# Layer 0's last three blocks and layer 3's last one: results added by one-hot matmuls instead of scatters

## The chip, the cores and the metric

The kernel runs on one core of a Trainium2 chip. The core has five engines with a queue of instructions each: TensorE (PE, with its weight loads as PEld), VectorE (DVE), ScalarE (ACT), GpSimd (POOL) and SyncE (SP). SP, ACT and POOL can start DMA transfers; 16 DMA engines carry them. The metric is the time of one execution on the device, in microseconds (us), lower is better. Times below that are not called medians come from one profiled execution and count from the start of its span.

## The reference

A model of four layers on 1024 tokens (4 sequences of 256) of width 256, all in float32. Each layer normalises the residual, adds a gated attention, normalises again, and adds a gated feed-forward part:

```python
x = x + tanh(g_xattn[0]) * L0_xattn(layernorm(x), ctx_512, ...)
x = x + tanh(g_ffn[0])   * L0_ffn(layernorm(x), ...)
...
x = x + tanh(g_xattn[3]) * L3_xattn(layernorm(x), ctx_512, ...)
x = x + tanh(g_ffn[3])   * L3_ffn(layernorm(x), ...)
```

Two of the feed-forward parts are mixtures of experts. Layer 0 has 16 experts of width 176 with 6 chosen for each token, and two shared ones; layer 3 has 8 experts of width 512 with 2 chosen, and one shared:

```python
# layer 0, for every expert
h = silu(x @ W1.T + B1) * (x @ W3.T + B3)
y = y + c[:, None] * (h @ W2.T + B2)      # c: the token's weight for this expert, or 0
# layer 1's feed-forward part: weights reduced to -1, 0 and 1
scale = mean(abs(w)); w_q = sign(w) * (abs(w) >= 0.7 * scale)
```

## The kernel before

The residual lies in SBUF as `stream`, 8 tiles of 128 tokens by 256 (`x[t]` is one). All steps are written one after the other and a scheduler places each engine's instructions.

**A mixture** (`ffn0`, `ffn3`) first routes: for each token and chosen expert it computes a place in a list sorted by expert, and cuts that list into blocks of 128 places, each with one expert. The class `Experts` runs over the blocks. For block `b`: `fetch` gathers 128 rows of the normalised tokens and their weights from DRAM with an indirect DMA on GpSimd (L1152); `turn` transposes them (L1164, copied by VectorE in L1165) and picks each row's weight (L1170); `up` multiplies with the expert's first weights (L1193, in layer 3 L1204), takes silu on ScalarE (L1212) and multiplies on VectorE (L1213); `turn_hidden` transposes the result (L1219, L1221); `down` multiplies with the second weights (L1228) and copies the result to one of 8 places of a ring in SBUF (L1237 on VectorE for odd blocks, L1239 on ScalarE for even ones). Then an indirect DMA on GpSimd adds the 128 rows to an accumulator in DRAM (L1240). Layer 0 alternates between two accumulators, `sums0[0]` (which starts as a copy of the residual) and `sums0[1]` (which starts as zero); layer 3 has one, `sums3[0]`. Two scatters to the same accumulator wait for one another.

`blocks` fetches four blocks ahead and keeps three blocks in work, so that in iteration `i` block `i` is turned, block `i-1` goes up and block `i-2` down; then it calls `between(i)`. Layer 0's `between` lets other work into the mixture: at every third iteration a step of `fold1` (TensorE folds weights of layer 1's attention, and the steps release weight buffers, so that the next loads start on SP), and after iteration 32 a step of `ternary1` (VectorE reduces and rounds the two weight matrices of layer 1's feed-forward part: eight `tensor_reduce` in L1462, a small matmul for the mean in L1472, then eight comparisons and eight selects in L1481 and L1482).

How many blocks there are depends on the data. 55 in layer 0 and 20 in layer 3 are sure; the rest stands behind a branch (`tc.If` on a value loaded in L1251). Every engine has its own copy of that branch, and on the path that skips the rest it raises its semaphores as if the rest had run; GpSimd does so for the scatters.

**After layer 0's mixture**, SP loads the first accumulator into `stream` (L1372) and ScalarE's queue loads the second into `more` (L1374), two loads of 512 KB each; VectorE adds them (L1377, four adds of two tiles); SP starts to load layer 3's expert weights once the adds are done; then layer 1's attention normalises the tiles (`layernorm`, L379 to L387), TensorE transposes them (L399) and projects them (L414, 16 projections of two matmuls), and softmax follows on VectorE, ScalarE and GpSimd (L420 to L430).

**At the end**, four copies from `sums3[0]` to the output, DRAM to DRAM, on SP and ScalarE (L1628).

`region`, `t4` and `small` take buffers of SBUF; `ps_mm` takes one of four PSUM banks.

Of the kernel before, what the change touches and what calls it, by code (L numbers as in the profile page):

```python
# [25 lines left out]
F32 = mybir.dt.float32  # L29
# [8 lines left out]
P = 128  # L38
# [27 lines left out]

NB0, NB3 = _blocks(E0, K0), _blocks(E3, K3)
SURE0, SURE3 = 55, 20
W0U = 4 * F0
W0, W3 = W0U + 2 * D, 4 * F3 + 4 * D  # L70
BIG = E3 * W3
# [10 lines left out]
def tile_flamingo(ctx: ExitStack, tc: tile.TileContext, a: dict, out: bass.AP):  # L82
# [291 lines left out]
    def layernorm(g):  # L374

        mv = small([P, TPG, 2], "mv")
        for i in range(TPG):
            st = small([P, 6], "st")
            nc.vector.bn_stats(st, x[g * TPG + i])  # L379
            nc.vector.bn_aggr(mv[:, i, :], st)  # L380
        rstd = small([P, TPG], "rstd")
        nc.scalar.activation(rstd, mv[:, :, 1], AF.Sqrt, bias=eps)  # L382
        nc.vector.reciprocal(rstd, rstd)
        xn = []
        for i in range(TPG):
            n = sb.tile([P, D], F32, tag="xn", name="xn", bufs=6)
            nc.vector.tensor_scalar(  # L387
                n, x[g * TPG + i], mv[:, i, 0:1], rstd[:, i : i + 1], ALU.subtract, ALU.mult
            )
            xn.append(n)  # L390
        return xn
# [432 lines left out]

    def attention1(gate):
        weff, wvo = kept.pop("fold1")
        qcT = latents()
        xT = [transposed(layernorm(0))]
        for g in range(NG):
            for pr in range(NP):  # L830
                if g == 0 and pr == NP // 2:
                    xT.append(transposed(layernorm(1)))
                ps = ps_mm()
                mm2(ps, lambda c: weff[:, c, pr * P : (pr + 1) * P], xT[g])
                evacuate(qcT[g][:, pr, :], ps)
        latent_attend(qcT, wvo, gate)


# [295 lines left out]
    class Experts:  # L1134


        def __init__(self, route, xd, n, nb, stride, width, chunk, sums, w, bias, hTs, between):
            self.gather, self.scatter, self.expert, self.offset, self.used = route
            self.xd, self.experts, self.nb, self.stride = xd, n, nb, stride
            self.width, self.chunk, self.n = width, chunk, width // chunk  # L1140
            self.sums, self.w, self.bias, self.hTs = sums, w, bias, hTs
            self.between = between
            self.ring = [sb.tile([P, 4, D], F32, tag="xT", name="ring", bufs=2) for _ in range(2)]
            self.weight: dict = {}
            self.xs: dict = {}
            self.at: dict = {}
            self.st: dict = {}
# [36 lines left out]
        def up(self, b):  # L1184
            st, r, n = self.st[b], self.at[b], self.width
            ps = ps_wide()
            s = st[:, D : D + n]
            if self.bias is not None:
                nc.tensor.matmul(
                    ps[:, 0, : 2 * n], self.bias[1][:, b : b + 1].to_broadcast([96, P]), self.bias[0], start=True, stop=False  # L1190
                )
                for c in range(2):
                    nc.tensor.matmul(  # L1193
                        ps[:, 0, : 2 * n],
                        st[:, c * P : (c + 1) * P],
                        self.w[:, bass.ds(r + c * 2 * n, 2 * n)],
                        start=False,
                        stop=(c == 1),
                    )
                gate, lin = ps[:, 0, :n], ps[:, 0, n : 2 * n]  # L1200
            else:
                for c in range(2):
                    for k in range(2):
                        nc.tensor.matmul(  # L1204
                            ps[:, k, :n],
                            st[:, c * P : (c + 1) * P],
                            self.w[:, bass.ds(r + (2 * c + k) * n, n)],
                            start=(c == 0),
                            stop=(c == 1),
                        )  # L1210
                gate, lin = ps[:, 0, :n], ps[:, 1, :n]
            nc.scalar.activation(s, gate, AF.Silu)  # L1212
            nc.vector.scalar_tensor_tensor(s, lin, self.weight.pop(b), s, ALU.mult, ALU.mult)  # L1213

        def turn_hidden(self, b):
            st, f = self.st[b], self.chunk
# [7 lines left out]
        def down(self, b):  # L1224
            (st, hT), r = self.st.pop(b), self.at.pop(b) + 4 * self.width
            ps = ps_mm()
            for j in range(self.n):
                nc.tensor.matmul(  # L1228
                    ps[:, :D],
                    hT[:, j * P : (j + 1) * P],  # L1230
                    self.w[: self.chunk, bass.ds(r + j * D, D)],
                    start=(j == 0),
                    stop=(j == self.n - 1),
                )
            y = self.ring[b // 4 % 2][:, b % 4, :]
            if b % 2:
                nc.vector.tensor_copy(y, ps[:, :D])  # L1237
            else:
                nc.scalar.copy(y, ps[:, :D])  # L1239
            nc.gpsimd.indirect_dma_start(  # L1240
                out=self.sums[b % len(self.sums)],
                out_offset=bass.IndirectOffsetOnAxis(ap=self.scatter[:, b : b + 1].bitcast(U32), axis=0),
                in_=y,
                in_offset=None,
                compute_op=ALU.add,
            )

        def run(self, sure):

            self.blocks(0, sure, self.between)  # L1250
            used = nc.values_load(self.used, min_val=0, max_val=self.nb)  # L1251
            with tc.If(used > sure):
                self.blocks(sure, self.nb, lambda i: None)

        def blocks(self, first, last, between):
            for b in range(first, min(first + 4, last)):
                self.fetch(b)
            for i in range(first, last + 2):
                if i + 4 < last:
                    self.fetch(i + 4)  # L1260
                if i < last:
                    self.turn(i)
                if i >= first + 2:
                    self.turn_hidden(i - 2)
                if first < i <= last:
                    self.up(i - 1)
                if i >= first + 2:
                    self.down(i - 2)
                between(i)

    def in_three(n, first, second, third):

# [5 lines left out]
    def ffn0(gate):  # L1278
# [60 lines left out]
        in_three(NT, up, turn, down)  # L1339
        for _ in steps:  # L1340
            pass
        used("L0_s13")
        used("L0_s2")
        keep_rows(sums0[0], 0)
        placing = route[1]
        expert = placing[2]
# [5 lines left out]

        fold = fold1()
        ended = []
        ternary = ternary1()

        def between(i):
            if i % 3 == 2 and not ended:
                try:
                    next(fold)  # L1360
                except StopIteration as end:
                    ended.append(end.value)
            if i > 32 and ended:
                next(ternary, None)

        moe = Experts(placing, xd, E0, NB0, W0, F0, FC0, sums0, big[:, : E0 * W0], (bias_0, choice), hTs, between)
        moe.run(SURE0)
        kept["fold1"] = ended[0]
        for t in range(NT):
            if t % TPG == 0:  # L1370
                tiles = slice(t, t + TPG)
                nc.sync.dma_start(out=stream[:, tiles, :], in_=tiled(sums0[0], 0)[:, tiles, :])  # L1372
                more = t4([P, TPG, D], "more")
                nc.scalar.dma_start(out=more, in_=tiled(sums0[1], 0)[:, tiles, :])  # L1374
            if t % 2 == 0:
                two, its = slice(t, t + 2), slice(t % TPG, t % TPG + 2)
                done = nc.vector.tensor_tensor(stream[:, two, :], stream[:, two, :], more[:, its, :], ALU.add)  # L1377
        load_experts3(0, EARLY3, done)
        for _ in ternary:
            pass  # L1380

    def ffn3(gate):
        normal = normalised()
# [53 lines left out]
        def hTs(st, b):  # L1437
            return hidden[:, (b % 4) * 512 : (b % 4 + 1) * 512]

        moe = Experts(route[0], xd, E3, NB3, W3, F3, P, sums3, big, None, hTs, lambda i: None)  # L1440
        moe.run(SURE3)


    def ternary(k):
# [10 lines left out]
    def ternary1():  # L1455
# [3 lines left out]
        for k in range(2):  # L1459
            part = small([P, 16], "part", 2)  # L1460
            for i in range(4):
                nc.vector.tensor_reduce(  # L1462
                    part[:, i * 4 : (i + 1) * 4],
                    loaded[f"L1_w{k + 1}"][:, i * 512 : (i + 1) * 512].rearrange("p (a b) -> p a b", a=4),
                    AX.X,
                    ALU.add,
                    apply_absolute_value=True,
                )
                yield
            nc.vector.tensor_reduce(sums[:, k : k + 1], part, AX.X, ALU.add)  # L1470
        ps = ps_mm()
# [149 lines left out]
        k = 4 * (i % 2) + i // 2  # L1621
        step(tg[:, k : k + 1])

    for i in range(4):
        rows = slice(i * T // 4, (i + 1) * T // 4)
        to, of = (v[rows].rearrange("(p r) d -> p (r d)", r=4) for v in (out, sums3[0]))
        engine = nc.scalar if i % 2 else nc.sync
        engine.dma_start(out=to, in_=of)  # L1628

def _rope(length, dim):
# [133 lines left out]
```

## Time and profile before

| | |
|---|---|
| median of 3 runs | 975.11 us (970.66, 975.11, 975.20) |
| profiled execution | 969.81 us |
| its span | 967.7 us |
| TensorE busy | 843.5 us (87%) |
| VectorE busy | 523.9 us (54%) |
| ScalarE busy | 274.1 us (28%) |
| GpSimd busy | 339.6 us (35%) |
| mean granted TensorE clock | 0.942 of full |

The rows of the profile read as follows. In a group, `out<-in` names the tiles by the program's names, then come shapes and the count; behind the first bar stand busy time and the mean of one in ns, behind the second the idle time of the engine just before and what ended it. In a timeline a row is start, length (us), engine, line, operation, tiles, count, and in brackets the idle time before it with its releaser. GpSimd's two kinds of work in layer 0's mixture:

```profile
L1240 POOL DMA_INDIRECT sums<-ring,big x55 | 87.8, 1596 | 34.4 <-issue 11.0
L1152 POOL DMA_INDIRECT xs<-xd,big x55 | 54.9, 999 | 55.9 <-DMA w_L_kv<-in_L_kv 35.5
```

The busy time of a group is a sum over all its instructions, whatever else runs beside them; a share of the span says nothing of whether the engine was waited for.

### The profile page before, as it was taken

The numbers are of one execution on the slowest core, as the hardware profiler recorded it, in microseconds if no ns is written. First come the engines' busy times: TensorE is split into PE (matmuls) and PEld (weight loads), VectorE is DVE, ScalarE is ACT, GpSimd is POOL, SyncE is SP. The second block draws the span as 40 slices with busy tenths as digits, with TensorE's granted clock in tenths as the row PEclk, the third lists the DMA queues.
The fourth block names the chain that finished last, engine by engine and source line by source line (L and its number), as shares of the span: only waits on it lengthen the run. The fifth ranks groups of instructions, "written<-read, shape, count | busy, mean of one in ns | idle before, by whom it ended". The sixth has DMA issues, their size and how long they took to land. (4 is left out here: it accounts for less than half of the span.)

```text
span 967.7 us, 12703 instructions
## 1 busy us (share of the span) xinstructions
PE 843.5 (87%) x4450; PEld 545.9 (56%) x4453; DVE 523.9 (54%) x1349; ACT 274.1 (28%) x531; POOL 339.6 (35%) x259
## 2 busy tenths in 40 slices
PE   5999999999999999984299987979647989999994
PEld 4544336876667866663147853835423556566662
DVE  4666557747833445361428745967796756222220
ACT  2122014443213232321113436134403441122221
POOL 0455552210157777886003124304201312144421
PEclk9999999999989999997599999988858999999998
DMA  9201137100266676554630000540000012122223
GB/s 346 96 16 39 60 123 220 33 28 9 77 150 161 127 169 149 86 83 57 231 121 1 1 1 0 184 154 2 22 1 1 1 44 52 45 45 44 39 22 66
DMA packets 38761, 75.14 MB, mean 78 GB/s; under 512 B 6240, under 2 KB 26706, under 8 KB 37322
## 3 DMA queue, kind: packets, MB, share of 16 engines
q1 hardware_dynamic: 23562, 52.01, 16.0%
q0 software_dynamic: 14496, 20.47, 13.2%
q10 hardware_dynamic: 640, 1.84, 0.5%
q8 instruction: 39, 0.64, 0.3%
q14 instruction: 24, 0.20, 0.1%
HBM read 58.73 MB, written 16.61 MB: 78 GB/s over the span
## 5 line engine op out<-in xcount | busy, mean ns | idle before, releaser
L430 POOL TENSOR_TENSOR attn<-attn,sm 128x1024 f32<-128x1024 f32 x32 | 60.8, 1901 | 242.3 <-DVE sm L429 224.3
L1213 DVE SCALAR_TENSOR_TENSOR blk<-wide,weight,blk 128x176 f32<-128x176 f32 (+1 forms) x75 | 37.0, 493 | 129.7 <-ACT blk L1212 122.8
L1240 POOL DMA_INDIRECT sums<-ring,big x55 | 87.8, 1596 | 34.4 <-issue 11.0
L414 PE MATMUL wide<-xT,big 128*128 128x512 f32 x192 | 87.9, 607 | 0.0
L675 DVE TENSOR_TENSOR rope<-wide,big 128x512 f32<-128x512 f32 x96 | 59.6, 684 | 48.3 <-PE wide L414 47.1
L1193 PE MATMUL wide<-big,blk 128*128 x220 | 76.1, 467 | 0.0
L1152 POOL DMA_INDIRECT xs<-xd,big x55 | 54.9, 999 | 55.9 <-DMA w_L_kv<-in_L_kv 35.5
L1204 PE MATMUL wide<-big,blk 128*128 x160 | 72.2, 593 | 0.5 <-DVE blk L1165 0.5
L399 PE MATMUL mm<-ident,xn 128*128 128x128 f32 x112 | 21.7, 342 | 52.7 <-DVE xn L387 40.4
L1212 ACT ACTIVATE blk<-wide 128x176 f32<-128x176 f32 (+1 forms) x75 | 29.5, 393 | 121.7 <-PE wide L1204 52.6
L414 PEld LDWEIGHTS wide<-xT,big 128*128 128x128 f32 x192 | 35.6, 193 | 47.1 <-issue 41.2
L648 PE MATMUL mm<-vo,attnT 128*128 128x256 f32 x256 | 58.8, 383 | 0.9 <-ACT attnT L445 0.9
L1228 PE MATMUL mm<-big,blk 88*128 x220 | 56.8, 380 | 1.2 <-DVE thr L1475 0.7
L445 ACT COPY attnT<-mm 128x512 f32<-128x512 f32 x64 | 34.9, 589 | 63.5 <-PE mm L444 63.5
L648 PEld LDWEIGHTS mm<-vo,attnT 128*128 128x128 f32 x256 | 47.4, 190 | 9.1 <-ACT attnT L445 3.3
L1228 PEld LDWEIGHTS mm<-big,blk 88*128 88x128 f32 x220 | 41.3, 189 | 16.6 <-ACT blk L1221 1.5
L399 PEld LDWEIGHTS mm<-ident,xn 128*128 128x128 f32 x112 | 16.2, 171 | 60.0 <-ACT rstd L382 33.0
L1193 PEld LDWEIGHTS wide<-big,blk 128*128 128x128 f32 x220 | 40.3, 194 | 13.1 <-issue 0.9
L428 DVE TENSOR_REDUCE sm<-attn 128x16 f32<-128x1024 f32 x32 | 38.9, 1215 | 14.7 <-ACT attn L422 12.6
L444 PE MATMUL mm<-ident,attn 128*128 128x128 f32 x256 | 35.7, 285 | 12.4 <-POOL attn L430 12.4
L449 DVE SCALAR_TENSOR_TENSOR x<-mm,tg,x 128x256 f32<-128x256 f32 x48 | 23.2, 482 | 42.1 <-PE mm L648 18.2
L1152 POOL DMA_INDIRECT xs<-xd,scratch x20 | 19.5, 975 | 74.8 <-PE mm L1164 54.2
(322 smaller groups left out, 1693.4 us busy)
## 6 DMA issues: line engine op xcount, KB each, us to landing
big<-in_L_w_gate_up SPq DMA_DIRECT2D x8, 1024.0 KB
big<-in_L_w SPq DMA_DIRECT2D x4, 1408.0 KB
big<-in_L_w_down SPq DMA_DIRECT2D x8, 512.0 KB
w_L_qk<-in_L_qk SPq DMA_DIRECT2D x4, 896.0 KB
big<-in_L_w SPq DMA_DIRECT2D x4, 704.0 KB
big<-in_L_wo SPq DMA_DIRECT2D x1, 2048.0 KB
xd<-xn SPq DMA_DIRECT2D x16, 128.0 KB
sums<-x SPq DMA_DIRECT2D x16, 128.0 KB
```

The lines of the kernel that those rows point to most:

```text
L399: nc.tensor.transpose(ps[:, i * P : (i + 1) * P], n[:, c * P : (c + 1) * P], ident)
L414: nc.tensor.matmul(ps, w(c), xT[:, c, :], start=(c == 0), stop=(c == 1))
L428: nc.vector.tensor_reduce(sm, e, AX.X, ALU.add)
L430: nc.gpsimd.tensor_tensor(e, e, sm.unsqueeze(2).to_broadcast([P, groups, n]), ALU.mult)
L648: nc.tensor.matmul(ps[:, :D], aT[:, s, :], vo[:, s, :], start=(s == 0), stop=(s == NP - 1))
L675: nc.vector.tensor_tensor(m[:, s, :].rearrange("q (b t) -> q b t", t=S), ps[:, s, :].rearrange("q (b t) -> q b t", t=S), table, ALU.mult,)
L1152: nc.gpsimd.indirect_dma_start(out=xs, out_offset=None, in_=self.xd, in_offset=bass.IndirectOffsetOnAxis(ap=self.gather[:, b : b + 1].bitc ...
L1193: nc.tensor.matmul(ps[:, 0, : 2 * n], st[:, c * P : (c + 1) * P], self.w[:, bass.ds(r + c * 2 * n, 2 * n)], start=False, stop=(c == 1),)
L1204: nc.tensor.matmul(ps[:, k, :n], st[:, c * P : (c + 1) * P], self.w[:, bass.ds(r + (2 * c + k) * n, n)], start=(c == 0), stop=(c == 1),)
L1213: nc.vector.scalar_tensor_tensor(s, lin, self.weight.pop(b), s, ALU.mult, ALU.mult)
L1228: nc.tensor.matmul(ps[:, :D], hT[:, j * P : (j + 1) * P], self.w[: self.chunk, bass.ds(r + j * D, D)], start=(j == 0), stop=(j == self.n - 1),
L1240: nc.gpsimd.indirect_dma_start(out=self.sums[b % len(self.sums)], out_offset=bass.IndirectOffsetOnAxis(ap=self.scatter[:, b : b + 1].bitca ...
```

## The change

The last blocks of the sure part are not scattered: in layer 0 the last three (`HOT0 = 3`: blocks 52, 53 and 54), in layer 3 the last one (`HOT3 = 1`: block 19). Their results stay in the ring. For each such block `hit` builds, on VectorE, a one-hot matrix for every tile of tokens (row of the block against token of the tile). After the branch `add` lets TensorE multiply these matrices with the results (8 tiles, one 128x128 by 128x256 matmul per tile and block, summed in PSUM over the blocks) and VectorE adds PSUM to `stream`. The accumulators are loaded by `collect`, which stands ahead of the branch. In layer 0 all four loads are now SP's. In layer 3 the accumulator is loaded back into `stream` in eight loads of one tile on SP and ScalarE, and the sums go from SBUF to the output in four stores. Blocks behind the branch are added in the same way, one at a time.

Three things move with it. `ternary1` leaves the mixture and is stepped in layer 1's attention, one step after each projection from the second half of the first group on, the rest after the last one; its reductions may not come sooner than the last normalised tile. `fold1` steps at every fourth iteration from 5 on instead of every third from 2 on. The release of layer 0's shared weights (`used`) moves from ahead of the mixture into iteration 3.

```diff
+HOT0, HOT3 = 3, 1
...
     def attention1(gate):
         weff, wvo = kept.pop("fold1")
+        ternary = ternary1()
...
                 evacuate(qcT[g][:, pr, :], ps)
+                if len(xT) == NG:
+                    next(ternary, None)
+        for _ in ternary:
+            pass
         latent_attend(qcT, wvo, gate)
...
         def down(self, b):
...
+            if b in self.hits:
+                self.held.append((self.hits.pop(b), y))
+                return
...
             nc.gpsimd.indirect_dma_start(
...
+        def hit(self, b, room, after=None):
+            base, step = self.rows
+            row, at = small([P, 1], "row"), small([P, NT], "at")
+            copied = nc.vector.tensor_copy(row, self.scatter[:, b : b + 1])
+            if after is not None:
+                behind(copied, after)
+            nc.vector.tensor_scalar(at, base, row, -1.0 / step, ALU.subtract, ALU.mult)
+            for h, first in room:
+                n = h.shape[1]
+                nc.vector.tensor_tensor(
+                    h,
+                    place.unsqueeze(1).to_broadcast([P, n, P]),
+                    at[:, first : first + n].unsqueeze(2).to_broadcast([P, n, P]),
+                    ALU.is_equal,
+                )
+            return room
+
+        def add(self, held, lo=0, hi=NT, done=lambda t: None):
+            for t in range(lo, hi, 2):
+                ps = ps_mm()
+                for u in (t, t + 1):
+                    for i, (hits, y) in enumerate(held):
+                        h = next(h[:, u - v, :] for h, v in hits if v <= u < v + h.shape[1])
+                        at = (u - t) * D
+                        nc.tensor.matmul(ps[:, at : at + D], h, y, start=(i == 0), stop=(i == len(held) - 1))
+                two = stream[:, t : t + 2, :]
+                nc.vector.tensor_tensor(two, ps.rearrange("p (u d) -> p u d", u=2), two, ALU.add)
+                done(t)
+
+        def run(self, sure, collect, done=lambda t: None):
+            self.sure = sure
+            self.blocks(0, sure, self.between, 4)
+            collect()
             used = nc.values_load(self.used, min_val=0, max_val=self.nb)
             with tc.If(used > sure):
-                self.blocks(sure, self.nb, lambda i: None)
+                self.blocks(sure, self.nb, lambda i: None, 1)
+            self.add(self.held, done=done)
...
-        used("L0_s13")
-        used("L0_s2")
         keep_rows(sums0[0], 0)
...
         def between(i):
-            if i % 3 == 2 and not ended:
+            if i == 3:
+                used("L0_s13")
+                used("L0_s2")
+            if i > 4 and i % 4 == 1 and not ended:
...
-            if i > 32 and ended:
-                next(ternary, None)
...
+        def collect():
+            more = [t4([P, TPG, D], "more") for _ in range(NG)]
+            groups = [slice(g * TPG, (g + 1) * TPG) for g in range(NG)]
+            for g in range(NG):
+                nc.sync.dma_start(out=stream[:, groups[g], :], in_=tiled(sums0[0], 0)[:, groups[g], :])
+            for g in range(NG):
+                nc.sync.dma_start(out=more[g], in_=tiled(sums0[1], 0)[:, groups[g], :])
+            for t in range(0, NT, 2):
+                two, its = slice(t, t + 2), slice(t % TPG, t % TPG + 2)
+                added.append(
+                    nc.vector.tensor_tensor(stream[:, two, :], stream[:, two, :], more[t // TPG][:, its, :], ALU.add)
+                )
...
+        def collect():
+            for t in range(NT):
+                engine = nc.scalar if t % 2 else nc.sync
+                engine.dma_start(out=x[t], in_=tiled(sums3[0], 3)[:, t, :])
+
+        def done(t):
+            engine = nc.scalar if t % 4 else nc.sync
+            rows = slice(t * P, (t + 2) * P)
+            engine.dma_start(out=out[rows].rearrange("(t p) d -> p t d", p=P), in_=stream[:, t : t + 2, :])
...
-    for i in range(4):
-        rows = slice(i * T // 4, (i + 1) * T // 4)
-        to, of = (v[rows].rearrange("(p r) d -> p (r d)", r=4) for v in (out, sums3[0]))
-        engine = nc.scalar if i % 2 else nc.sync
-        engine.dma_start(out=to, in_=of)
```

## The prediction

> **What bounds the kernel now.** I read the windows first, then the timeline across the hole that they show, then GpSimd's own queue, then the last microseconds. The windows (length, busy time of each engine with its instructions, granted TensorE clock, DMA share, GB/s) show that around the end of layer 0's mixture TensorE does nothing:
>
> ```profile
> 440.00:450.00 10.00, 7.61 (x34) 4.93 (x32) 2.38 (x6) 2.81 (x8) 6.11 (x4) 0.98 0.44 48
> 450.00:460.00 10.00, 0.00 (x0) 0.00 (x0) 0.00 (x0) 0.00 (x0) 6.29 (x5) 0.50 0.48 54
> 476.00:481.00 5.00, 4.20 (x12) 2.54 (x13) 3.56 (x12) 0.89 (x2) 0.00 (x0) 0.57 1.04 403
> 480.00:490.00 10.00, 10.00 (x31) 4.89 (x30) 2.08 (x3) 2.35 (x4) 0.00 (x0) 0.99 1.04 389
> ```
>
> The timeline fills the hole: TensorE's last expert matmul ends at 448.1 and its next starts at 476.77.
>
> ```profile
> 446.99 1.13 PE L1228 MATMUL mm<-big,blk 88*128 x4 [0.46 <-ACT blk L1221]
> 448.54 1.55 POOL L1240 DMA_INDIRECT sums<-ring,big  x1 [1.79 <-ACT ring L1239]
> 450.39 1.55 POOL L1240 DMA_INDIRECT sums<-ring,big  x1 [0.30 <-issue]
> 453.22 1.55 POOL L1240 DMA_INDIRECT sums<-ring,big  x1 [1.28 <-issue]
> 455.07 1.55 POOL L1240 DMA_INDIRECT sums<-ring,big  x1 [0.30 <-issue]
> 457.82 1.55 POOL L1240 DMA_INDIRECT sums<-ring,big  x1 [1.20 <-DMA sums<-ring,big]
> 463.32 0.81 SPq L1372 DMA_DIRECT2D x<-sums  x2
> 463.47 0.84 ACTq L1374 DMA_DIRECT2D more<-sums  x2
> 469.68 1.29 DVE L1377 TENSOR_TENSOR x<-x,more 128x512 f32<-128x512 f32 x2 [23.13 <-DMA more<-sums]
> 472.18 1.29 DVE L1377 TENSOR_TENSOR x<-x,more 128x512 f32<-128x512 f32 x2 [0.54 <-DMA more<-sums]
> 476.77 2.09 PE L399 MATMUL mm<-ident,xn 128*128 128x128 f32 x8 [28.64 <-DVE xn L387]
> ```
>
> The scatters are those of blocks 50 to 54. They lag because GpSimd, not TensorE, sets the pace: in mid-mixture a gather (0.99) and a scatter (1.59), each with 0.30 of issue, make 3.2 us a block, and the ring copy of block 51 stands at 440.82 while its scatter is issued at 450.39. Scatters to one accumulator follow each other by 4.6 (453.22 to 457.82). So the hole is: queue of scatters, landing, loads, two adds, layernorm.
>
> At the end of the program the same thing in small:
>
> ```profile
> 953.11 1.55 POOL L1240 DMA_INDIRECT sums<-ring,scratch  x1 [4.18 <-ACT ring L1239]
> 957.61 1.55 POOL L1240 DMA_INDIRECT sums<-ring,scratch  x1 [2.95 <-DMA sums<-ring,scratch]
> 961.38 1.20 SPq L1628 DMA_DIRECT2D out_dram<-sums  x2
> ```
>
> **The change part by part.** *Last scatters of layer 0.* In the changed program's GpSimd order 10 gathers lead the scatters and 7 scatters follow the last gather, where 10 did; the work up to block 51 is the same. Its scatter stays at 450.39: -7.4 against 457.82. At the start the weight fold leaves iteration 2 (1.97 us of TensorE at 278.1); GpSimd's 0.74 idle before its gather at 282.83, put down to TensorE, goes with some of its wait for the first ring copy: -1 (0 to -2).
>
> *Loads.* Before, SP's loads stood behind the branch, whose skipped path lets GpSimd raise the scatters' semaphores only after the last landing: 5.5 from the issue at 457.82 to 463.32. Now they stand ahead of it and wait for their own scatter: 4.5 by the 4.6 between scatters of one accumulator, less a hop. x is asked for at 448.54 + 4.5 - 1 = 452.0, the second accumulator at 450.39 + 4.5 - 1 = 453.9, all four on SP, ScalarE's two among them. Nothing else waits on SP: the expert weights behind them want the adds in both programs. Before, the four (2 MB) took 463.32 to 472.1, 8.8. From 452.0 that gives 460.8 as the late bound; the second pair alone at the 389 GB/s of the 480 to 490 window (1 MB, 2.7 us, and some 1.4 to a first packet) gives 458.0 as the early one. I take 460.0.
>
> *The branch.* The built order puts the four adds of the two accumulators ahead of VectorE's branch and the matmuls behind it with a wait for VectorE's count, so TensorE cannot start early: last add dispatched at 460.6, then the branch, 0.65 to 1.3 (VectorE's load of the flag starts at 446.2 and its skipped path ends at 447.4; in layer 3 955.5 to 956.1). TensorE starts at 461.7.
>
> *One-hot matmuls.* 3 blocks x 8 tiles = 24 of 128x128 by 256. Eight of that shape (L1228) take 1.73 at full clock, 0.216 each, so 0.43 at the granted 0.50. The clock here was full again 3.4 us after the first matmul (0.57 in 476 to 481, 0.99 after), so of the 12 for the first four tiles 8 are slow (3.4) and 4 fast (0.9): 466.0. The add from PSUM is like L1411's 690 ns: 466.7. The other 12 (2.6) run beside the layernorm. Layernorm of the first four tiles behind it: two statistics 0.75, two aggregates 0.24, root 0.30, reciprocal 0.14, the third add standing in VectorE's order 0.69, first normalised tile 0.42, hops 0.4: 469.7 for the first transpose against 476.77, -7.1. TensorE is warm by then, but VectorE's copy of the second half xT now stands behind the fourth add and two statistics: I give the warm clock 0.3 of its 1.7. **Layer 0: -7.4** (-11 to -3, from the bounds of loads, branch and start, and 3 us for a DMA collision as at 384.98 below).
>
> *One-hot matrices.* Three 128x1024 comparisons, not in the trace; the nearest row is L421's 1219 ns, the far one two L1462 of 681. They stand in the mixture's VectorE (4 of 10 us busy) while scatters lag by 10 us: nothing. Without that lag, some 4 us.
>
> *Ternary weights move to layer 1's attention.* 8 reductions of 0.681, 8 comparisons of 0.482, 8 selects of 0.748: 15.3 us of VectorE. Under the 28 us of projections (2.08 of 10 us busy, 480 to 490) they are covered. But the threshold needs all eight reductions and a small matmul, which stands behind projection 13 of 16; after it 8 pairs of 1.23 remain. By the built order 6 pairs, four evacuations and a half pair stand ahead of the first softmax maximum, and another pair and a half inside the first two softmaxes. From the threshold VectorE reaches that maximum after 0.45 + 7.9 + 2.75 = 11.1; TensorE has its scores after three projections (5.2) and 4.0, so 9.1 (512.08 before). 2.0 late, and 1.5 more inside:
>
> ```profile
> 512.08 1.23 DVE L420 TENSOR_REDUCE mx<-wide 128x16 f32<-128x1024 f32 x1 [1.23 <-PE wide L633]
> 513.34 1.22 DVE L421 TENSOR_TENSOR attn<-wide,mx 128x1024 f32<-128x1024 f32 x1
> 516.20 1.22 DVE L421 TENSOR_TENSOR attn<-wide,mx 128x1024 f32<-128x1024 f32 x1
> 517.34 1.21 DVE L428 TENSOR_REDUCE sm<-attn 128x16 f32<-128x1024 f32 x1
> ```
>
> VectorE works without a gap here, and GpSimd's product and the transposes wait for L428: **+3.5** (+1 to +5).
> What leaves the mixture there was hidden: GpSimd's stalls of about 2.8 at 363.00 and 384.98 follow the loads of the ternary weights (issued 356.49 and 376.31), which stay.
>
> *Layer 3.* Scatter 18 lands at 956.9 instead of 19 at 961.3. But eight loads of 128 KB follow, four on each queue, about 0.42 to issue, in by 961.8 (at the program's start 512 KB landed some 3 us after issue; 1 MB goes at the same pace). ScalarE passes its branch after its four loads, 959.4, and TensorE waits for its count; four pairs of cold matmuls run to 963, the last add to 963.7, the last store goes then, 256 KB, some 3 us: 966.7 against 966.3 where the copy's last packet ended. **+0.4** (-0.7 to +2).
>
> [...]
>
> Sum: -7.4 + 3.5 + 0.4 = **-3.5**. The profiled execution took 969.81 (span 967.7): 966.3. The three timed runs have 970.66, 975.11 and 975.20, so it is among the short ones; a median may fall 4 to 5 higher. I say **968**.
>
> **The rivals.** *The ternary work gives it back, and more.* If VectorE's 15.3 us lie on the path, because the threshold comes late and projections then wait for evacuations behind it, the sum is -7.4 + 15.3 + 0.4 = +8.3: 978. It decides once more than 7.0 of the 15.3 are uncovered. For it: the chain of waits runs over VectorE at 512 to 518; against: 28 us of cover, and eight reductions fit in 7 us.
> *The loads hide it.* If the two accumulators' loads land no sooner than GpSimd's backlog lets them, say because the second ternary weight and the layer 2 load, now after iteration 45, collide with the last scatters (2.8 as at 384.98), and their bandwidth holds the late bound (0.8), layer 0 is -3.8 and the sum +0.1: 970, no difference.
> *The mixture gains too.* If the two stalls of 2.5 each above the usual 0.3 came from the reductions waiting on VectorE and not from the loads, scatter 51 comes 5 earlier: -8.5, 961. For it: VectorE did wait for both weights; against: ring copies ran 9.6 us ahead of the scatter at 384.98.
>
> **How the numbers follow.** Forecast 0.48 (its own range 963 to 973), mixture gain 0.17, hidden 0.20, given back 0.15. Half a per cent, 4.9 us, is about what a measurement of this kernel tells from no change. Below 970.2 lie the mixture gain and most of the forecast (0.38): 0.55. Within: the rest of the forecast and the hidden case: 0.30. Slower: 0.15. The range reaches from 958 to 977.
>
> **What would show it.** The scatter of block 51 within 3 of 449.4, SP's loads at 452 to 454 (right), TensorE's first one-hot matmul at 461.7 at clock 0.50, the first L399 transpose at 469.7; from there to the first softmax sum 3.5 more than the 40.6 of before. Wrong if scatters shift by over 3, if the matmuls do not wait for the adds, or if projections stall.

## The result and the profile after

No difference that can be measured. The changed kernel took 973.32 us (median) against 971.59 for the kernel before, a ratio of 1.0016 (95% interval 0.9995 to 1.0036). In a second comparison on another chip it was 970.81 against 971.34, 0.9998 (0.9980 to 1.0017). One execution of the changed kernel, at 1149.88 us and a granted clock of 0.735, is left out of the ratio. The range of 958 to 977 holds the result; the forecast (3.5 us less, a median of 968) did not come. The profiled execution took 973.33 (span 971.5, before 967.7).

The windows of the changed kernel around the end of layer 0's mixture (length, busy time of each engine with its instructions, granted TensorE clock, DMA share, GB/s):

```profile
440.00:450.00 10.00, 6.25 (x26) 3.75 (x24) 1.44 (x4) 3.67 (x8) 5.75 (x4) 0.87 0.51 58
450.00:460.00 10.00, 0.00 (x0) 0.00 (x0) 2.50 (x4) 0.00 (x0) 0.00 (x0) 0.50 0.66 219
460.00:470.00 10.00, 7.67 (x23) 6.33 (x24) 1.66 (x5) 0.00 (x0) 0.00 (x0) 0.60 0.91 327
470.00:480.00 10.00, 9.72 (x43) 7.08 (x42) 8.08 (x26) 1.44 (x4) 0.00 (x0) 1.00 0.82 304
```

TensorE's hole is shorter, but what follows it is not attention yet. The timeline across it (start, length, engine, line, operation, and in brackets the idle time ahead with its releaser):

```profile
445.63 1.13 PE L1239 MATMUL mm<-big,blk 88*128 x4 [0.46 <-ACT blk L1232]
...
447.11 1.55 POOL L1261 DMA_INDIRECT sums<-ring,big  x1 [1.15 <-DMA sums<-ring,big]
...
448.40 0.82 SPq L1438 DMA_DIRECT2D x<-sums  x2
452.59 0.81 SPq L1440 DMA_DIRECT2D more<-sums  x2
457.40 2.50 DVE L1444 TENSOR_TENSOR x<-x,more 128x512 f32<-128x512 f32 x4 [12.22 <-DMA more<-sums]
462.33 13.37 PE L1295 MATMUL mm<-ring,hits 128*128 128x256 f32 x48 [15.57 <-DVEq L1306]
467.83 0.69 DVE L1297 TENSOR_TENSOR x<-mm,x 128x512 f32<-128x512 f32 x1 [7.93 <-PE mm L1295]
...
470.56 0.69 DVE L1297 TENSOR_TENSOR x<-mm,x 128x512 f32<-128x512 f32 x1 [1.04 <-PE mm L1295]
...
475.54 1.04 PE L401 MATMUL mm<-ident,xn 128*128 128x128 f32 x8
```

Read it from both ends. The last scatter goes 10.7 earlier (447.11, before 457.82) and both loads are issued by 453.4, as the change means to. But the code issues 24 one-hot matmuls, and the trace has x48 in 13.37 us. From the end of the last expert matmul to the first transpose of layer 1's attention it is 28.8 (446.76 to 475.54), as before (448.12 to 476.77: 28.7): 13 us of idle TensorE became 13 us of one-hot matmuls. The granted clock over their first part (third from the end) is a half up to 468, 5.6 us after the first of them:

```profile
460.00:464.00 4.00, 1.67 (x4) 1.43 (x5) 0.00 (x0) 0.00 (x0) 0.00 (x0) 0.50 0.69 233
464.00:468.00 4.00, 4.00 (x11) 3.13 (x11) 0.17 (x1) 0.00 (x0) 0.00 (x0) 0.51 1.05 400
468.00:472.00 4.00, 4.00 (x20) 3.54 (x19) 2.90 (x9) 0.00 (x0) 0.00 (x0) 1.00 1.04 381
```

In layer 1's attention, on VectorE:

```profile
509.84 0.74 DVE L1598 SCALAR_TENSOR_TENSOR w_L_w<-w_L_w,thr,low 128x512 bf16<-128x512 f32 x1
510.61 0.48 DVE L1597 TENSOR_SCALAR low<-w_L_w,nthr 128x512 f32<-128x512 f32 x1
511.02 1.22 DVE L422 TENSOR_REDUCE mx<-wide 128x16 f32<-128x1024 f32 x1
512.15 0.74 DVE L1598 SCALAR_TENSOR_TENSOR w_L_w<-w_L_w,thr,low 128x512 bf16<-128x512 f32 x1
512.81 1.21 DVE L423 TENSOR_TENSOR attn<-wide,mx 128x1024 f32<-128x1024 f32 x1
513.94 0.47 DVE L1597 TENSOR_SCALAR low<-w_L_w,nthr 128x512 f32<-128x512 f32 x1
...
517.27 1.21 DVE L430 TENSOR_REDUCE sm<-attn 128x16 f32<-128x1024 f32 x1
```

The ternary selections (L1597, L1598) stand ahead of the first softmax maximum and inside the softmax. And at the end of the program:

```profile
954.27 1.55 POOL L1261 DMA_INDIRECT sums<-ring,scratch  x1 [3.99 <-ACT ring L1252]
...
959.22 1.75 SPq L1526 DMA_DIRECT2D x<-sums  x4
959.22 1.81 ACTq L1526 DMA_DIRECT2D x<-sums  x4
...
961.67 5.98 PE L1295 MATMUL mm<-ring,hits 128*128 128x256 f32 x16 [4.92 <-ACTq L1306]
963.79 0.69 DVE L1297 TENSOR_TENSOR x<-mm,x 128x512 f32<-128x512 f32 x1 [6.57 <-PE mm L1295]
...
967.70 0.69 DVE L1297 TENSOR_TENSOR x<-mm,x 128x512 f32<-128x512 f32 x1 [0.17 <-PE mm L1295]
```

Eight matmuls again show as x16, the first 4.5 us of them at a granted clock of 0.50, and the last add ends 14.1 after the scatter.

The 3.8 between the two spans, by stages:

| stage | before | after | difference |
|---|---|---|---|
| to the end of layer 0's last expert matmul | 448.12 | 446.76 | -1.4 |
| to the first attention transpose (the hole) | 28.65 | 28.78 | +0.1 |
| to the matmul behind the last projection (L617) | 31.34 | 30.08 | -1.3 |
| to the first softmax sum (L430) | 9.23 | 11.65 | +2.4 |
| to the first transpose of the layer's next part | 53.76 | 55.40 | +1.6 |
| to the scatter of layer 3's block 18 | 382.01 | 381.60 | -0.4 |
| to the end of the span (the tail) | 14.59 | 17.23 | +2.6 |

### The profile page after: what moved, and what is told of

It reads as the page before. It is cut to its first block, busy times and chain, and to the rows that moved or that the text cites. A ratio compares the mean times of both kernels' runs of the same rounds, so it can differ in the third digit from the quotient of the medians.

```text
span 971.5 us, 12908 instructions
## 1 busy us (share of the span) xinstructions
PE 861.2 (89%) x4517; PEld 559.5 (58%) x4517; DVE 534.2 (55%) x1370; ACT 273.6 (28%) x531; POOL 334.1 (34%) x255
## 5 line engine op out<-in xcount | busy, mean ns | idle before, releaser
L1261 POOL DMA_INDIRECT sums<-ring,big x52 | 83.3, 1603 | 28.9 <-DVE own L1181 9.1
L1204 PEld LDWEIGHTS wide<-big,blk 128*128 128x128 f32 x220 | 40.0, 193 | 12.8 <-issue 0.5
L430 DVE TENSOR_REDUCE sm<-attn 128x16 f32<-128x1024 f32 x32 | 38.9, 1214 | 14.8 <-ACT attn L424 12.4
L1215 PEld LDWEIGHTS wide<-big,blk 128*128 128x128 f32 x160 | 28.8, 190 | 28.9 <-issue 28.2
L1261 POOL DMA_INDIRECT sums<-ring,scratch x19 | 29.9, 1574 | 36.1 <-ACT ring L1252 16.6
```

Source lines behind the costliest of these rows:

```text
L430: nc.vector.tensor_reduce(sm, e, AX.X, ALU.add)
L1204: nc.tensor.matmul(ps[:, 0, : 2 * n], st[:, c * P : (c + 1) * P], self.w[:, bass.ds(r + c * 2 * n, 2 * n)], start=False, stop=(c == 1),)
L1215: nc.tensor.matmul(ps[:, k, :n], st[:, c * P : (c + 1) * P], self.w[:, bass.ds(r + (2 * c + k) * n, n)], start=(c == 0), stop=(c == 1),)
L1261: nc.gpsimd.indirect_dma_start(out=self.sums[b % len(self.sums)], out_offset=bass.IndirectOffsetOnAxis(ap=self.scatter[:, b : b + 1].bitca ...
```

## The experiments

My theory after the result was: a float32 one-hot matmul is two records of the trace, so it costs twice what I counted; the ternary work costs some 2.4 in attention; layer 3 loses some 2.6. The rivals: loads and branch set the start whatever the matmuls cost; or the ternary work alone gives everything back.

**One of three blocks added.**

```diff
-            self.add(self.held, done=done)
+            self.add(self.held[-1:], done=done)
```

> Layer 0 adds only the last of its three held blocks by one-hot matmuls; the other two blocks' results are left out, all else as in the changed kernel. Theory (price: a float32 one-hot matmul runs as two passes, 0.43 us each at half clock and 0.216 at full, so 24 of them take 13.4 us where 6.9 were counted, and the first 12 of them lie on the path): the first two pairs of tiles need 8 passes instead of 24, 3.4 us instead of some 8.2, so the first transposes of layer 1's attention move from 475.5 to about 470.7, with x16 records in place of x48, and the program becomes 3 to 5 faster than the changed kernel, near 969. Rival (loads and branch set the start, the matmuls hide in the wait): first transposes within 1 of 475.5. Rival (ternary work on VectorE is what gives it back): first transposes 4.8 earlier, but the first softmax sum within 1 of 517.3 and the program within 1 of 973.3.

```profile
461.79 5.92 PE L1295 MATMUL mm<-ring,hits 128*128 128x256 f32 x16 [15.34 <-DVEq L1306]
471.66 2.10 PE L401 MATMUL mm<-ident,xn 128*128 128x128 f32 x8 [3.96 <-DVE xn L389]
```

Eight matmuls are x16 records, and the transposes come 3.9 earlier (the hole is 25.2). The matmuls are on the path; the rival of loads and branch falls. The first softmax sum came only 1.7 earlier (515.57). That is not the ternary work, since the stretch from the last projection to it is 11.6 as in the changed kernel: TensorE stood idle for 3.96 ahead of the transposes, its granted clock was 0.50 again by 470, and from the first transposes to the last projection it took 32.3 instead of 30.1. The program's time, 1004.66, says nothing about the change: without two blocks the later layers see other data, and layer 3's mixture used three blocks more than the 20 that stand ahead of its branch (954 to 993 in the trace).

**Layer 0's matmuls ahead of the loads' adds and of the branch**, into four PSUM banks; VectorE then adds them pair by pair with the loads.

```diff
             collect()
+            if early:
+                self.add(self.held)
+                early()
             used = nc.values_load(self.used, min_val=0, max_val=self.nb)
...
-            self.add(self.held, done=done)
+            if not early:
+                self.add(self.held, done=done)
```

> Layer 0's 24 one-hot matmuls stand ahead of the loads' adds and of the branch, into four PSUM banks, so that they run while the accumulators are being loaded; the same arithmetic. Theory (price): they start at about 449.5, right behind the last expert matmul, run 10 to 13 us beside the loads, the eight adds end near 463.3, and the first transposes come at 467.5 (2 either way) instead of 475.5; the program becomes 5 to 8 faster than the changed kernel, 965 to 968, if VectorE's ternary work does not take it back. Rival (loads and branch set the end): first transposes not before 473. Rival (ternary work takes it back): first transposes near 467.5, but the first softmax sum within 2 of 517.3, program 971 or more.

```profile
448.44 10.53 PE L1295 MATMUL mm<-ring,hits 128*128 128x256 f32 x48
...
462.38 0.69 DVE L1453 TENSOR_TENSOR x<-x,more 128x512 f32<-128x512 f32 x1
...
466.24 0.75 DVE L381 BATCH_NORM_STATS2 st<-x 128x6 f32<-128x256 f32 x2 [3.17 <-DVEq L1309]
...
470.28 2.10 PE L401 MATMUL mm<-ident,xn 128*128 128x128 f32 x8 [11.31 <-DVE xn L389]
```

The same 48 records take 10.53 right behind the experts, where the clock is still full: 0.219 each, 0.44 for a matmul; 13.37 in the changed kernel is the same work with its first part at half clock. The hole falls from 28.8 to 21.7. The transposes are later than the 467.5 I expected: the mixture ended 1.8 later than in the changed kernel's profile, and VectorE needs 3.2 past the skipped branch. Part of the gain is lost again behind it: TensorE is idle for 11.31 ahead of the transposes, the clock is 0.77 over 470 to 480, and from the first transposes to the last projection it takes 32.0 instead of 30.1. Program 970.22, 0.9975 of before (0.9952 to 0.9998), where I had expected 965 to 968.

**Two blocks instead of three, and the ternary work in the mixture again.**

```diff
-HOT0, HOT3 = 3, 1
+HOT0, HOT3 = 2, 1
```

> Two blocks of layer 0 instead of three go by one-hot matmuls, one more by the scatter queue; ternary work in layer 1's attention as in the changed kernel. Theory (price): the last scatter and the loads come 2 to 2.5 later, 8 passes fewer lie ahead of the first transposes (8 x 0.22 to 0.43 = 1.7 to 3.4), so the first transposes stay within 1.5 of 475.5 and the program within 1.5 of the changed kernel's 973. Rival (matmuls hide in the waits): first transposes 2 to 2.5 later and the program 975 to 976.

The hole is 27.6, 1.1 less than with three (0.6 less than in the changed kernel's second profile); one more scatter and 8 matmuls fewer nearly cancel. (The first transposes stand at 470.8 because this execution's mixture began 3.5 earlier.) The program, 974.99 and 1.0034 (1.0011 to 1.0058), is a little slower than the kernel before and than I expected, but not to be told from the changed kernel's first ratio. For the second kernel of the pair `between` steps the ternary generator again and attention does not:

```diff
-                if len(xT) == NG:
-                    next(ternary, None)
...
+            if i > 32 and ended:
+                next(ternary, None)
```

> As the kernel with two blocks, but the ternary work of layer 1's weights runs in layer 0's mixture again, as before the change. It tells the price of moving it. Theory (a small tax, +1 to +4): the time from the first transposes of layer 1's attention to its first softmax sum falls by 1 to 3.5, and the program becomes 1 to 4 faster than the kernel with two blocks. Rival (the ternary work is covered by the projections): no difference, within 0.7. Rival (it holds up the mixture's gathers and scatters): the last scatter of the layer comes 2 or more later than in the kernel with two blocks and the program is not faster.

From the last projection to the first softmax sum it is 9.23, as before the change, where two blocks alone have 11.63. But it is not a clean price: the weight fold steps every fourth block here, where it stepped every third, so the small matmul for the threshold came only at 470.65 and the threshold at 471.46, and the selections ran on into the projections, which took 33.3 instead of 30.7. Program 972.53, 1.0014 (0.9987 to 1.0041): overlapping, so the expected gain isn't shown. The scatters were not held up (187.4 from the first gather to the last scatter, 188.4 without).

**Layer 3 as before**, with its scatters and the copy at the end (`HOT3 = 0` and the old copies).

> The changed kernel with layer 3 as it was before (all blocks scattered, the output copied from the accumulator); layer 0 and the ternary work as changed. Theory (16 passes at half clock, behind ScalarE's branch, cost layer 3 some 2.6): from the next to last scatter (block 18) to the end of the span 14.6 as before the change instead of 17.2, and the program 2 to 3 faster than the changed kernel, 970 to 971. Rival (layer 3 is neutral, as forecast at +0.4): 17.2 again or no more than 0.7 less, program 973.

Program 970.01, 0.9986 (0.9966 to 1.0006); the tail is 15.54, not 14.6, since the last scatter here was issued 5.6 after block 18's and before the change 4.5. One tail is not a price; over the profiles with the changed layer 3 it was 17.2, 18.5, 18.3, 17.7, 16.7 and 17.6, with scatters 14.6, 15.5 and 16.7. By the means (17.7 and 15.6) the one-hot way costs layer 3 some 2; the two sets touch at 16.7, and the program's interval holds 1, so this is a reading of the traces and no measured gain.

**The eight ternary reductions in the wait for the loads**, threshold and selections where the change has them.

```diff
         def collect():
+            kept["normal"] = moe.copied
+            ternary = kept["ternary"] = ternary1()
+            for _ in range(8):
+                next(ternary)
...
```

> The changed kernel with the eight absolute-sum reductions of the ternary weights put on VectorE ahead of layer 0's loads' adds, where it idles; threshold and selection stay with the projections. Theory (the late threshold pushes 2.4 of VectorE work between the last projection and the first softmax sum): that stretch is 9.2 again, as before the change, instead of 11.65; TensorE's pause of 1.30 ahead of the second half of the scores goes; the first transposes stay at 475.5; the program 1 to 3 faster than the changed kernel, 970 to 972. Rival (the stretch is set by something else): 11.65 again, program 973.

```profile
504.72 0.69 DVE L136 COPY vo<-mm 128x512 f32<-128x512 f32 x1 [0.38 <-PE mm L617]
505.58 0.69 DVE L136 COPY vo<-mm 128x512 f32<-128x512 f32 x1 [0.17 <-PE mm L617]
507.51 1.23 DVE L422 TENSOR_REDUCE mx<-wide 128x16 f32<-128x1024 f32 x1 [1.23 <-PE wide L635]
508.77 1.22 DVE L423 TENSOR_TENSOR attn<-wide,mx 128x1024 f32<-128x1024 f32 x1
...
512.77 1.21 DVE L430 TENSOR_REDUCE sm<-attn 128x16 f32<-128x1024 f32 x1
```

VectorE waits for TensorE's scores again, no selection stands between, and the stretch is 9.23. TensorE's pause of 1.30 is gone. Program 968.42, 0.9974 (0.9945 to 1.0003). So the +2.4 of this stretch comes from the late threshold; it was not the whole loss, and the program's interval still holds 1.

**All of it together**: the early matmuls, the reductions in the wait, and layer 3 as before; then the same with layer 3's one-hot matmuls ahead of its loads and branch. The order of layer 0's adds differs from the early matmuls above: VectorE adds three of the four pairs of sums to the first accumulator while the second is on its way, where it went pair by pair.

> Layer 0's one-hot matmuls ahead of loads and branch, the reductions in the wait for the loads, and layer 3 as before the change. Theory: first transposes near 469, last projection to first softmax sum 9.2, layer 3's tail 14.6: 6.9 + 2.4 + 2.6 = some 10 to 12 off the changed kernel's 973, less a pause or two more of TensorE's clock: 962 to 965, below both kernels. Rival (stages further on take it back): 968 or more.

> As the kernel before it, but layer 3 too adds its last block by one-hot matmuls that stand ahead of its loads and of the branch. Theory: the 16 passes run at full clock while the loads are under way, the four adds follow the landing, and the tail from the scatter of block 18 is about 14.0 (4.95 to the loads' issue, 2.5 to land, 2.8 of adds, 3.2 to 3.7 for the stores): within 1 of the kernel with layer 3 as before. Rival (loads and stores in a row cost more than one copy): tail 15.5 or more.

Both are faster than both kernels, by under 1%: 965.12, 0.9926 (0.9902 to 0.9951), and 962.64, 0.9903 (0.9877 to 0.9929). The hole is 19.1 and 18.9 (21.7 with the adds pair by pair), the stretch to the softmax sum 9.2. The first has a tail of 16.7 (its last scatter went 6.1 after block 18's). For the second I expected 14.0 and got 16.7, the rival's side:

```profile
946.54 1.55 POOL L1261 DMA_INDIRECT sums<-ring,scratch  x1 [3.99 <-ACT ring L1252]
...
949.54 3.72 PE L1295 MATMUL mm<-ring,hits 128*128 128x256 f32 x16 [0.52 <-DVE ring L1250]
...
953.73 1.37 DVE L1297 TENSOR_TENSOR x<-mm,x 128x512 f32<-128x512 f32 x2 [4.25 <-DMA x<-sums]
955.71 1.43 DVE L1297 TENSOR_TENSOR x<-mm,x 128x512 f32<-128x512 f32 x2 [0.61 <-DMA x<-sums]
957.48 1.80 SPq L1549 DMA_DIRECT2D out_dram<-x  x2
```

The matmuls now take 3.72 at full clock, out of the way. But the first two pairs are done at 955.1, and no store goes before 957.48, 0.34 behind the last add. So either the branch, which stands between adds and stores, holds them, or the transfers would end no sooner anyway.

**The stores ahead of the branch** (and once more inside it), with the kernel above and the changed kernel beside it on the same chip.

```diff
                 early()
+                for t in range(0, NT, 2):
+                    done(t)
             used = nc.values_load(self.used, min_val=0, max_val=self.nb)
```

> The kernel e8_best_b with layer 3's four stores ahead of its branch (and once more inside it, for the case that it is taken). In e8_best_b the first pair of adds ended at 954.4 and all four stores were issued at 957.48, 0.34 behind the last add, waiting for VectorE's way past the branch. Theory (the branch holds the stores): the first store goes within 1 of the first adds, the tail from the scatter of block 18 falls from 16.66 to about 14, program 959.5 to 961.5. Rival (the transfers themselves set the end: stores to one output land one after the other): tail 16 or more, program within 1 of that kernel.

> The kernel e8_best_b on the same chip as its neighbours here, for a comparison of like with like: 961 to 964.

> The changed kernel itself on the same chip: 971 to 975, within 0.4% of the kernel before. From the first gather of layer 0 to the first transposes 215.3, from the last projection to the first softmax sum 11.65, tail from the scatter of block 18 17.2, as in its first profile; where TensorE's clock falls to a half after the pauses at 516 to 521 may differ.

```profile
947.07 2.85 DVE L1297 TENSOR_TENSOR x<-mm,x 128x512 f32<-128x512 f32 x4 [4.45 <-DMA x<-sums]
947.79 1.95 SPq L1551 DMA_DIRECT2D out_dram<-x  x2
948.54 1.80 ACTq L1551 DMA_DIRECT2D out_dram<-x  x2
```

With the stores first, the first one goes 0.72 behind the start of the first add, and the tail is 14.4 (954.1 less 939.68), against 16.5 in the repeat of the kernel above and 18.5 in the changed kernel: the branch held the stores. Program 960.81, 0.9911 (0.9879 to 0.9942); the repeat of the kernel above 964.62, 0.9927 (0.9910 to 0.9945), a little over what I expected of it. The tail tells these two apart, the programs' times do not. Against the changed kernel (970.81, 0.9998) both gain, by intervals that do not overlap. In its repeat the changed kernel has a hole of 28.2 and again 11.64 to the softmax sum.

## Why the prediction was right in places and missed the forecast

- *The scatters*: right within the 3 us allowed, in part by luck. Block 51's was forecast at 449.4 and stands at 447.11, 3.3 before its place in the kernel before. Of these, 2.3 were won after the first gather, where I had said 1. The other 1.0 is a first gather that came earlier (260.28, before 261.24), which I had not forecast; over the profiles here it stands anywhere from 256.8 to 262.0.
- *The loads*: right in what counts, with errors that cancel. Asked for at 448.40 and 452.59 (said 452.0 and 453.9), the four adds over at 459.9 (said 460.6). The second was asked for 5.5 after its scatter, where I had 4.5, and the early scatter made up for it. The first accumulator's 3.6 were worth nothing, since the adds wait for the second.
- *The branch*: 1.1 said, 2.4 measured (459.9 to 462.33), and 3.0 to 3.8 for VectorE in the kernels with early matmuls. The early adds made up for it: 461.7 said, 462.33 measured.
- **The one-hot matmuls: the step that failed.** "Eight of that shape (L1228) take 1.73 at full clock, 0.216 each": the eight are records, not matmuls. The code issues two matmuls a block at that line in layer 0, and the timeline shows x4 a block (in layer 3 four, and x8); I had both before me and did not compare them. A matmul is 0.44 at full clock (10.53 for the 24 early ones). The clock was mis-sized too: half for 3.4 us was said, and it was half for 5.6 (three other profiles of the same matmuls at the same place have 3.2 to 4.2). Of the 24, the first 12 were to end at 466.0; the add of the second pair began at 470.56. Of these 4.6 an estimated 2.6 are the count and 1.1 the clock, and 0.6 the later start. The third pair, which stands ahead of the normalised tile in VectorE's order, was late for the same reasons. So -7.1 became -1.2 at the first transposes, and +0.1 counted as a hole.
- *The warm clock*: 0.3 said, 1.3 measured (31.34 to 30.08): behind the longer run of matmuls the clock was full (1.00) from the first projection to the last.
- *The ternary work*: +3.5 said, +2.4 measured, by the mechanism given (late threshold, selections ahead of and inside the softmax); the reductions in the wait took it back whole. The rival that it costs 15.3 falls.
- *Layer 3*: +0.4 said, +2.6 between the two profiles, about 2 by the means above. The same mis-sized term is part of it: "four pairs of cold matmuls" with the last add were to take 4.3 (959.4 to 963.7) and took 6.7 (961.67 to 968.4); and the loads were issued 4.95 after the scatter where I had 3.8. How the 2 divide between the two was not tested.
- *The mixture gains too* falls: with the reductions out of the mixture GpSimd still stands idle for 3.35, 4.44 and 1.85 ahead of the scatters at 310.18, 345.07 and 423.21, and from the first gather to the last expert matmul it is 186.5 against 186.9. *The loads hide it* gave the right outcome, no difference, by a mechanism that did not happen: the loads were early.
- *Not in the forecast*: +1.6 in attention, below; the changed kernel's second profile does not have it (53.8).

## What to carry to other kernels

Before a row of the trace prices a new instruction, divide its count by what the code issues at that line; a float32 matmul here is two records (x48 for 24) and 0.44 us for 256 columns at full clock (10.53 for 24). Work that needs only data already there belongs ahead of the wait, not behind it: the same 48 records stood in the hole for 13.4 behind the loads, and ahead of them the hole is 7 to 10 shorter. What came behind the longer idle stretch has to be counted against that: from the first transposes to the last projection it took 30.1 after the late matmuls, at a clock of 1.00 over 470 to 480, and 31.6 to 33.0 after the early ones, where TensorE had been idle for 8.5 to 11.3 and the clock of the first of these kernels was 0.77 over the same stretch. A branch that is never taken was a wait here as well: 2.4 to 3.8 for the engine, and for the stores queued behind it a tail of 16.5, against 14.4 with the stores ahead of it.

## What the chip showed that I had not expected

TensorE's clock fell to a half after pauses of some two microseconds in six of the thirteen profiles here, and stayed full after such pauses in the other seven. In the changed kernel's first profile it paused 1.30 and 1.93 at 516 to 521, and then:

```profile
521.00:522.00 1.00, 0.56 (x5) 0.56 (x6) 1.00 (x2) 0.00 (x0) 0.39 (x1) 1.00 0.00 0
522.00:523.00 1.00, 0.76 (x6) 0.52 (x5) 1.00 (x2) 0.86 (x2) 0.00 (x0) 0.78 0.06 16
523.00:524.00 1.00, 1.00 (x3) 0.82 (x4) 1.00 (x3) 1.00 (x2) 0.52 (x1) 0.50 0.00 0
524.00:525.00 1.00, 1.00 (x3) 0.80 (x3) 1.00 (x2) 0.25 (x1) 1.00 (x1) 0.50 0.00 0
525.00:526.00 1.00, 1.00 (x4) 0.75 (x3) 1.00 (x2) 0.00 (x0) 0.39 (x1) 0.52 0.00 0
526.00:527.00 1.00, 1.00 (x6) 0.90 (x5) 0.64 (x1) 0.00 (x0) 0.00 (x0) 1.00 0.00 0
```

The clock (third from the end) is at a half for some 3.4 us, by the 0.78, 0.50, 0.50 and 0.52 of these rows, and this is the +1.6 of the table: that stage took 55.1 to 55.4 in the six profiles whose clock fell there, and 53.8 to 53.9 in the seven where it stayed at 1.00, the kernel before and the changed kernel's second profile among them. The pauses alone do not tell the two apart. Of six profiles with pauses of 1.30 and 1.93 the clock fell in four; of six with one pause of 2.15 it fell in two (e8_best_b and e4_hot2_mix); after the 2.06 of the kernel before it stayed. What decides whether it falls is not shown by any run. Nor did I take apart what the 2.4 to 3.8 of a skipped branch consist of, and why the last two scatters of layer 3 stand 4.5 apart in one execution and 6.1 in another is open.
